# Pairwise distances in a graph layer: from two small matmuls on TensorE to squares on ScalarE and sums on GpSimd, with the messages one graph later

## The chip, the cores and the metric

The kernel runs on one core of one Trainium2 chip. The metric is the device time of one execution in microseconds. Before the change the median of three runs is 2149.64 us (2147.59 to 2150.93).

## The reference

Input x is 64 graphs of 256 nodes with 256 features (fp32), adj is 64 dense 256 x 256 adjacency matrices. Two layers follow each other, each with a residual sum and a layer norm. The first normalizes adj by its row sums and computes (norm_adj + alpha I) x W^T + b. The second, cut to what matters here:

```python
h = relu(bn(conv1d_1tap(x)))                 # 256 -> 256
h = bn(conv1d_17taps(h))                     # along the nodes
x_conv = relu(h + x)
s = x @ w_se.T + b_se                        # three numbers a node
dist = sq[:, :, None] + sq[:, None, :] - 2 * s @ s.T
A = exp(-dist) * adj
msg = relu(x @ w_msg.T + b_msg)
x_nmp = A @ msg
out = GRU(input=[x_conv, x_nmp], state=x)    # w_ih (768 x 512), w_hh (768 x 256)
```

A layer norm of x + out ends it. dist[n, m] is the squared Euclidean distance of two points with three coordinates each.

## The kernel before

**Stages.** The 64 graphs are taken in four quarters of 16. In the setup stage (to about 284 us) the first quarter's graphs pass through both layers up to the GRU's inputs, beside the preparation of the transformed weights of the 17-tap convolution (`weights`). The convolution runs as a real transform of length 48 in tiles of 32 nodes, for a quarter at once: `p_dft` (L480) transforms each graph, `products` multiplies per frequency with u tiles loaded from memory (L539, `load_u` on SyncE), then `real_transform`, `complex_begin` and `complex_end` transform back on VectorE and `output` writes xc_d. Then the GRU (`gates`, `gru`, L832 on) reads three things for each graph from memory: the convolution's result, x1 and xn_d, which holds x1 transposed in its first half and the messages transposed in its second.

While one quarter's products, inverse transform and GRU run, the next quarter's graphs are begun: `open_ahead` holds V2, a buffer for the transforms of the first 12 (later 6) graphs of that quarter, whose own place VM is still in use. They are copied over by `copies` (L1052).

**One graph.** `graphs` (L960) starts the loads of the graph three ahead, and interleaves three generators piece by piece: `layer1` of this graph, `layer0` of the graph two later (adjacency transposes and degrees; p_hT at L399; p_out at L409 with the layer norm) and `others` (weights, or pieces of a GRU). `PLACES` says which of the other two gets a piece after which piece of layer1. The pieces of layer1 are: x1 transposed (L428), `p_conv` with bias and relu into h (L443 to L447; columns 256 to 258 of h are s), `p_msg` (L464), `p_dft` (L480), the rows, the distances with the product, and the messages.

**The distances.** VectorE copies s four times into `scols` (128 columns, of which 3 and a constant one or the halved negative square sum are used), TensorE transposes both chunks (p_rows, L493), ScalarE and VectorE copy 64 rows each out (`dist_l` L495, `dist_r` L497), TensorE multiplies 32 rows of one with 32 of the other (p_dist, L504), and ScalarE takes exp(2 p + bias) with the negative square sum as bias (L505). VectorE multiplies by the adjacency (L506) and TensorE multiplies by msg (p_nmp, L513). ScalarE copies that into the second half of xn, and one transfer of 512 KB writes xn (L518).

**Order.** The framework's scheduler orders each engine's instructions by a model of when their inputs are ready, and by the order in which the program was traced among those that are. The queues are then fixed: each engine takes its instructions in that order and waits where one isn't ready. Buffers are slots of a pool (`bufs=`): a new tile waits until the readers of the slot's last tile are done. `issue_after` forces an order by hand, and `paced` (L942) uses it: after each instruction given to `mark` it queues pieces of the inverse transform at the rates of L1042, so many per mark. In the first quarter `take(begin, 3)` (L1079) advances the next quarter's graphs by three pieces for each of the 12 steps of the products, before `paced` takes the rest.

## Time and profile before

| | before |
|---|---|
| median of three runs | 2149.64 us |
| the profiled execution's span | 2152.3 us |
| TensorE busy (PE) | 2052.7 us, 9693 matmuls |
| VectorE busy (DVE) | 1581.6 us |
| ScalarE busy (ACT) | 841.9 us |
| GpSimd busy (POOL) | 664.8 us |
| DMA | 298.30 MB, mean 139 GB/s |
| mean granted TensorE clock | 0.990 |

The profile is of one execution, whose span is 2.7 us above the median of the timed runs. A line of the groups reads: line of the kernel, engine, operation, written tile <- read tiles, shapes (partitions x elements), count | busy us, mean ns of one | the engine's idle time just before the group and what ended most of it. A span of a matmul holds its tail, which overlaps the next one, so the mean of a single one is longer than the distance from start to start. In a table of stages the columns are the stretch, its length, and for each engine the busy time and the count, then the granted clock, the DMA engines' mean busy share and GB/s. Timelines give start, length, engine, line, operation, tiles, shapes and count.

### The profile page before, as it was taken

How to read it: one execution, taken by the hardware profiler on the slowest of the kernel's cores; microseconds unless marked ns; L12 is line 12 of the kernel's file. 1: busy time of each engine (PE TensorE's matmuls, PEld its weight loads, DVE VectorE, ACT ScalarE, POOL GpSimd, SP SyncE). 2: the span in 40 equal slices, each digit the busy share in tenths (PEclk: the TensorE clock that was granted, in tenths of full speed). 3: DMA queues.
4: the chain of work that ended last, by engine and by line, in shares of the span. 5: the costliest groups of instructions: out<-in, count | busy, mean ns of one | idle time of the engine just before them, and what ended most of it. 6: DMA issues, size and time to landing. Idle time of an engine off the chain costs nothing.

```text
span 2152.3 us, 28977 instructions
## 1 busy us (share of the span) xinstructions
PE 2052.7 (95%) x9693; PEld 1735.8 (81%) x9693; DVE 1581.6 (73%) x3719; ACT 841.9 (39%) x1857; POOL 664.8 (31%) x640
## 2 busy tenths in 40 slices
PE   7999999887999999899999999999999998999997
PEld 5888788776888888788888888777888887788886
DVE  5555578775568788775656988876566889988887
ACT  4665643456431123445552122446553112222222
POOL 2444310121431244213322133323231123444442
PEclk9999999999999999999999999999999999999999
DMA  4766666434346644233326654324324744443331
GB/s 122 235 196 197 198 194 207 142 132 134 96 146 203 203 110 128 93 112 113 113 94 190 205 157 113 118 98 133 102 88 136 243 116 122 119 102 99 94 84 54
DMA packets 295085, 298.30 MB, mean 139 GB/s; under 512 B 76414, under 2 KB 273618, under 8 KB 294938
## 3 DMA queue, kind: packets, MB, share of 16 engines
q1 hardware_dynamic: 235050, 200.46, 30.9%
q10 hardware_dynamic: 44480, 67.39, 8.8%
q0 software_dynamic: 15408, 28.61, 6.1%
q8 instruction: 77, 1.26, 0.2%
q14 instruction: 70, 0.57, 0.1%
HBM read 193.28 MB, written 103.06 MB: 138 GB/s over the span
## 4 chain that ended last, share of the span: by engine, by line
PE 44%; DVE 12%; issue 9%; POOL 6%; ACT 4%; DMA 2%; ACTq 0%; SPq 0%; POOLq 0%; DVEq 0%
PE p_rz L846 14%; PE p_n L883 8%; PE p_k L539 7%; PE p_out L409 2%; PE p_nmp L513 2%; PE p_hT L399 2%; PE p_dft L480 2%; POOL ln_rs L323 2%; PE p_conv L443 1%; PE p_msg L464 1%; PE p_dist L504 1%; POOL sums L826 1%; POOL sums L825 1%; DMA u<-ud 1%; POOL xc_g L796 1%
## 5 line engine op out<-in xcount | busy, mean ns | idle before, releaser
L883 PE MATMUL p_n<-wn,inputs 128*128 128x256 f32 x1536 | 355.1, 385 | 13.4 <-DVE first L859 13.2
L846 PE MATMUL p_rz<-wrz,sums 128*128 128x256 f32 x1536 | 348.6, 380 | 1.3 <-DVE gn L888 0.8
L883 PEld LDWEIGHTS p_n<-wn,inputs 128*128 128x128 f32 x1536 | 288.5, 192 | 64.2 <-DVE first L859 20.9
L846 PEld LDWEIGHTS p_rz<-wrz,sums 128*128 128x128 f32 x1536 | 290.0, 190 | 44.5 <-issue 5.2
L846 PE MATMUL p_rz<-wrz,inputs 128*128 128x256 f32 x1152 | 271.6, 379 | 1.0 <-ACT inputs L808 1.0
L323 POOL TENSOR_TENSOR ln_rs<-ln_rs,neg_half 128x2 f32<-128x2 f32 x129 | 99.1, 768 | 510.9 <-DVE ln_rs L322 464.0
L846 PEld LDWEIGHTS p_rz<-wrz,inputs 128*128 128x128 f32 x1152 | 217.6, 190 | 31.1 <-ACT inputs L808 1.2
L895 ACT ACTIVATE nn<-gn 128x256 f32<-128x256 f32 x128 | 53.3, 417 | 332.1 <-DVE gn L892 331.7
L539 PE MATMUL p_k<-u,VM 128*128 128x256 f32 x736 | 175.2, 380 | 2.7 <-DMA u<-ud 1.9
L369 POOL TENSOR_TENSOR dis<-deg,neg_half 128x2 f32<-128x2 f32 x64 | 46.1, 720 | 423.6 <-DVE deg L367 393.1
L333 ACT ACTIVATE x_g<-x_g,ln_mr,ln_rs 128x256 f32<-128x256 f32 x128 | 70.0, 593 | 241.5 <-DVE ln_mr L331 241.5
L539 PEld LDWEIGHTS p_k<-u,VM 128*128 128x128 f32 x736 | 138.1, 190 | 24.4 <-DMA u<-ud 4.1
L480 PE MATMUL p_dft<-fwd,h 128*128 128x240 f32 x512 | 120.2, 379 | 25.9 <-ACT h L447 24.6
L399 PE MATMUL p_hT<-adjT,x 128*128 128x256 f32 x512 | 129.8, 397 | 14.0 <-DVE adjT L381 7.6
L825 POOL TENSOR_TENSOR sums<-inputs 128x384 f32<-128x384 f32 x64 | 67.1, 1048 | 239.0 <-ACT inputs L816 206.3
L480 PEld LDWEIGHTS p_dft<-fwd,h 128*128 128x128 f32 x512 | 95.2, 192 | 47.6 <-ACT h L447 41.2
L506 DVE TENSOR_TENSOR aT<-aT,adjT 128x512 f32<-128x512 f32 x64 | 44.6, 698 | 118.2 <-ACT aT L505 118.1
L443 PE MATMUL p_conv<-wc,xn 128*128 128x259 f32 x512 | 125.8, 388 | 4.3 <-ACT xn L429 4.3
L392 POOL TENSOR_TENSOR x_t<-x_t,b_t 128x512 f32<-128x512 f32 x64 | 85.4, 1334 | 142.6 <-ACT x L391 97.4
L409 PE MATMUL p_out<-w,hT 128*128 128x256 f32 x512 | 123.1, 383 | 1.4 <-ACT hT L404 0.7
L464 PE MATMUL p_msg<-wmsg,xn 128*128 128x256 f32 x512 | 121.4, 380 | 0.0
L513 PE MATMUL p_nmp<-aT,msg 128*128 128x256 f32 x512 | 121.2, 379 | 0.2 <-DVE aT L506 0.2
(157 smaller groups left out, 3910.2 us busy)
## 6 DMA issues: line engine op xcount, KB each, us to landing
u<-ud SPq DMA_DIRECT2D x284, 256.0 KB
xn_d<-xn ACTq DMA_DIRECT2D x64, 512.0 KB
inputs<-xn_d SPq DMA_DIRECT2D x64, 512.0 KB
ud<-u_set POOLq DMA_DIRECT2D x39, 480.0 KB, 6.1
adj_t<-in_adj_dram SPq DMA_DIRECT2D x64, 256.0 KB
x_t<-in_x_dram SPq DMA_DIRECT2D x64, 256.0 KB
x_d<-x ACTq DMA_DIRECT2D x64, 256.0 KB
xc_d<-VM SPq DMA_DIRECT2D x64, 256.0 KB
```

The costliest lines, as they stand in the source:

```text
L323: nc.gpsimd.tensor_tensor(rs[:, : len(chunks)], rs[:, : len(chunks)], neg_half[:, : len(chunks)], op=ALU.pow)
L392: nc.gpsimd.tensor_tensor(x_t, x_t, b0_t.unsqueeze(1).to_broadcast([P, NCH, D]), op=ALU.add)
L399: nc.tensor.matmul(p[:, k, :], x1[:, mc, k * P : (k + 1) * P], adjT[:, mc, 1 - mc : 3 - mc, :].rearrange("p n q -> p (n q)"), start=mc == ...
L409: nc.tensor.matmul(p[:, c, :], hT[:, k, c * P : (c + 1) * P], w0[:, k, :], start=k == 0, stop=k == DCH - 1)
L443: nc.tensor.matmul(p, x1T[:, k, c * P : (c + 1) * P], wc1[:, k, :], start=k == 0, stop=k == DCH - 1)
L464: nc.tensor.matmul(p[:, c, :], x1T[:, k, c * P : (c + 1) * P], wmsg[:, k, :], start=k == 0, stop=k == DCH - 1)
L480: nc.tensor.matmul(p[:, t0 * FL : t1 * FL], h[:, c, k * P : (k + 1) * P], fwd[:, first : first + t1 - t0, :].rearrange("p t f -> p (t f)") ...
L513: nc.tensor.matmul(p[:, k, :], msg[:, mc, k * P : (k + 1) * P], aT[:, mc].rearrange("p n q -> p (n q)"), start=mc == 0, stop=mc == NCH - 1,)
L539: nc.tensor.matmul(p[:, j * D : (j + 1) * D], v[:, k, :], u[:, k, :], start=k == 0, stop=k == DCH - 1)
L825: nc.gpsimd.tensor_tensor(S[:, 0], A21, A22, op=ALU.add)
L846: nc.tensor.matmul(p[:, j * D : (j + 1) * D], a[:, k], wrz[:, b, k], start=k == 0, stop=k == HALF - 1)
L883: nc.tensor.matmul(p[:, o * D : (o + 1) * D], lhsT, w, start=j == 0, stop=j == len(part) - 1)
```

## The change

The distances are computed directly as a sum of three squares. The three s columns of a graph are copied out of h (`own`), written to memory (s_d, 3 KB) and read back to all 128 partitions as one row of 256 x 3 (`everyone`, 384 KB in all). For each coordinate d and each half of the nodes ScalarE computes (own - everyone)^2 with own as bias and scale -1, six activations of 128 x 256, reading every third element. GpSimd adds the second and the third coordinate to the first. ScalarE takes exp(-aT), VectorE multiplies by the adjacency as before. scols, its transposes, the copies, p_dist and the square sums are gone.

The product with msg runs in the next graph's layer1 (`messages`, after that graph's p_msg), and for the last graph in `graphs`. There x1 of the next graph is transposed too, for every graph (before: only for graphs in ALONE, the others at the beginning of their own layer1). xn is split into x1T and nmp, written by two transfers, both issued by ScalarE's queue.

layer1 has four pieces instead of seven, and PLACES has four entries. Buffers: adjT 4 instead of 3, msg 2 instead of 1, turn 2 instead of 3; V2 of the later quarters holds 5 graphs instead of 6. `everyone`, `aT`, `square` and `nmp` have one buffer each.

```diff
--- before.py
+++ after.py
@@ -140,10 +140,6 @@
     nc.vector.tensor_scalar(alpha_t, alpha_t, MIN_ALPHA, None, op0=ALU.max)
 
 
-    scols = const.tile([P, NCH, P], F32, name="scols")
-    nc.gpsimd.memset(scols, 0.0)
-    for c in (NSE, 32 + NSE):
-        nc.gpsimd.memset(scols[:, :, c : c + 1], 1.0)
 
 
 
@@ -338,8 +334,8 @@
     xc_d = [dram.tile([Q, N, D], F32, name=f"xc_d{q}") for q in range(NQ)]
     x1_d = [dram.tile([Q, N, D], F32, name=f"x1_d{q}") for q in range(NQ)]
     xn_d = [dram.tile([P, 2 * DCH, N], F32, name=f"xn_d{g}") for g in range(B)]
-    XN = {}
-    ALONE = set()
+    s_d = [dram.tile([N, NSE], F32, name=f"s_d{g}") for g in range(B)]
+    X1T, NMP = {}, []
     ADJT, X1, X_SCALED, DIAGONAL = {}, {}, {}, {}
 
 
@@ -347,7 +343,7 @@
 
         a_t, x_t = ain.pop(g), xin.pop(g)
 
-        adjT = work.tile([P, NCH, 3, P], F32, name="adjT", bufs=3)
+        adjT = work.tile([P, NCH, 3, P], F32, name="adjT", bufs=4)
         ADJT[g] = adjT
 
         deg = small.tile([P, NCH], F32, name="deg")
@@ -420,21 +416,58 @@
         yield
 
     def x1_transposed(g):
+        if g >= B:
+            return
         x1 = X1.pop(g)
-        xn = XN[g] = work.tile([P, 2 * DCH, N], F32, name="xn")
+        x1T = X1T[g] = work.tile([P, DCH, N], F32, name="x1T")
         p = bank("p_x1T").rearrange("p (k n) -> p k n", k=DCH)
         for k in range(DCH):
             for c in range(NCH):
                 nc.tensor.transpose(p[:, k, c * P : (c + 1) * P], x1[:, c, k * P : (k + 1) * P], ident)
-        nc.scalar.copy(xn[:, :DCH], p)
+        nc.scalar.copy(x1T, p)
+        nc.scalar.dma_start(xn_d[g][:, :DCH], x1T)
+
+    def adjacency(g, own, adjT, msg):
+
+
+        everyone = work.tile([P, N, NSE], F32, name="s_all", bufs=1)
+        nc.sync.dma_start(s_d[g].rearrange("(c p) s -> p c s", p=P), own)
+        flat = s_d[g].rearrange("n s -> (n s)")
+        nc.sync.dma_start(everyone, bass.AP(tensor=flat.tensor, offset=flat.offset, ap=[[0, P], [NSE, N], [1, NSE]]))
+        yield
+        aT = work.tile([P, NCH, N], F32, name="aT", bufs=1)
+        for d in range(NSE):
+            to = aT if d == 0 else work.tile([P, NCH, N], F32, name="square", bufs=1)
+            for c in range(NCH):
+                nc.scalar.activation(
+                    to[:, c], everyone[:, :, d], AF.Square, bias=own[:, c, d : d + 1], scale=-1.0
+                )
+            if d:
+                nc.gpsimd.tensor_tensor(aT, aT, to, op=ALU.add)
+        nc.scalar.activation(aT, aT, AF.Exp, scale=-1.0)
+        blocks_of = aT.rearrange("p c (n q) -> p c n q", q=P)
+        mark(nc.vector.tensor_mul(blocks_of, blocks_of, adjT[:, :, 0:3:2, :]))
+        NMP.append((g, aT, msg))
+
+    def messages():
+        if not NMP:
+            return
+        g, aT, msg = NMP.pop(0)
+        p = bank("p_nmp").rearrange("p (k n) -> p k n", k=DCH)
+        for k in range(DCH):
+            for mc in range(NCH):
+                nc.tensor.matmul(
+                    p[:, k, :], msg[:, mc, k * P : (k + 1) * P], aT[:, mc], start=mc == 0, stop=mc == NCH - 1,
+                )
+        nmp = work.tile([P, DCH, N], F32, name="nmp", bufs=1)
+        nc.scalar.copy(nmp, p)
+        nc.scalar.dma_start(xn_d[g][:, DCH:], nmp)
 
     def layer1(g, place):
 
-        if g not in XN:
+        if g not in X1T:
             x1_transposed(g)
-        xn, adjT = XN.pop(g), ADJT.pop(g)
-        x1T = xn[:, :DCH]
-        yield
+        x1T, adjT = X1T.pop(g), ADJT.pop(g)
 
         h = work.tile([P, NCH, D + NSE], F32, name="h", bufs=1)
         for c in range(NCH):
@@ -444,20 +477,13 @@
                     p, x1T[:, k, c * P : (c + 1) * P], wc1[:, k, :], start=k == 0, stop=k == DCH - 1
                 )
             mark(nc.vector.tensor_tensor(h[:, c, :], p, bc1, op=ALU.add))
+        own = small.tile([P, NCH, NSE], F32, name="own")
+        nc.vector.tensor_copy(own, h[:, :, D:])
         nc.scalar.activation(h[:, :, :D], h[:, :, :D], AF.Relu)
-
-        s3 = h[:, :, D:]
-        cols = scols.rearrange("p c (q r) -> p c q r", r=32)
-        nc.vector.tensor_copy(cols[:, :, :, :NSE], s3.unsqueeze(2).to_broadcast([P, NCH, 4, NSE]))
-        sq3 = small.tile([P, NCH, NSE], F32, name="sq3")
-        nc.vector.scalar_tensor_tensor(sq3, s3, -1.0, s3, op0=ALU.mult, op1=ALU.mult)
-        nsq = small.tile([P, NCH], F32, name="nsq")
-        nc.vector.tensor_reduce(nsq, sq3, AX.X, ALU.add)
-        nc.vector.tensor_scalar(
-            cols[:, :, 2:4, NSE], nsq.unsqueeze(2).to_broadcast([P, NCH, 2]), 0.5, None, op0=ALU.mult
-        )
-        yield
-        msg = work.tile([P, NCH, D], F32, name="msg", bufs=1)
+        msg = work.tile([P, NCH, D], F32, name="msg")
+        weighing = adjacency(g, own, adjT, msg)
+        next(weighing)
+        yield
         p = bank("p_msg").rearrange("p (c d) -> p c d", c=NCH)
         for c in range(NCH):
             for k in range(DCH):
@@ -466,6 +492,9 @@
                 )
         mark(nc.vector.tensor_tensor(msg, p, bmsg_t.unsqueeze(1).to_broadcast([P, NCH, D]), op=ALU.add))
         nc.scalar.activation(msg, msg, AF.Relu)
+        yield
+        messages()
+        x1_transposed(g + 1)
         yield
 
 
@@ -486,36 +515,7 @@
                 TILES[0][:, :, k, place * GT : (place + 1) * GT],
                 p[:, : GT * FL].rearrange("p (t f) -> p f t", f=FL),
             )
-
-        yield
-        p = bank("p_rows")
-        for c in range(NCH):
-            nc.tensor.transpose(p[:, c * P : (c + 1) * P], scols[:, c, :], ident)
-        dl = work.tile([64, N], F32, name="dist_l", bufs=1)
-        nc.scalar.copy(dl, p[0:64, :N])
-        dr = work.tile([64, N], F32, name="dist_r", bufs=1)
-        nc.vector.tensor_copy(dr, p[64:P, :N])
-        yield
-
-        aT = work.tile([P, NCH, 2, P], F32, name="aT", bufs=1)
-        for c in range(NCH):
-            rows = slice(32 * c, 32 * c + 32)
-            p = bank("p_dist")[:, :N]
-            nc.tensor.matmul(p, dl[rows, c * P : (c + 1) * P], dr[rows, :], start=True, stop=True)
-            nc.scalar.activation(aT[:, c].rearrange("p n q -> p (n q)"), p, AF.Exp, bias=nsq[:, c : c + 1], scale=2.0)
-        mark(nc.vector.tensor_mul(aT, aT, adjT[:, :, 0:3:2, :]))
-        yield
-        if g in ALONE:
-            x1_transposed(g + 1)
-        p = bank("p_nmp").rearrange("p (k n) -> p k n", k=DCH)
-        for k in range(DCH):
-            for mc in range(NCH):
-                nc.tensor.matmul(
-                    p[:, k, :], msg[:, mc, k * P : (k + 1) * P], aT[:, mc].rearrange("p n q -> p (n q)"),
-                    start=mc == 0, stop=mc == NCH - 1,
-                )
-        nc.scalar.copy(xn[:, DCH:], p)
-        nc.scalar.dma_start(xn_d[g], xn)
+        run(weighing)
         yield
 
 
@@ -633,7 +633,7 @@
     def turned(re, im, angle):
 
 
-        t = freq.tile([P, 2, D], F32, name="turn", bufs=3)
+        t = freq.tile([P, 2, D], F32, name="turn", bufs=2)
         x, y = M[:, re, :], M[:, im, :]
         real_part(t[:, int(re > im), :], x, y, angle)
         return imaginary_part(t[:, int(re < im), :], x, y, angle), t
@@ -661,7 +661,7 @@
         nc.vector.tensor_add(M[:, 12, :], M[:, 4, :], M[:, 12, :])
         for i, x, y in ((1, 9, 13), (2, 10, 14), (3, 15, 11)):
             angle = math.pi * ORDER[i] / 8
-            t = freq.tile([P, 2, D], F32, name="turn", bufs=3)
+            t = freq.tile([P, 2, D], F32, name="turn", bufs=2)
             by = real_part(t[:, 0, :], M[:, x, :], M[:, y, :], angle)
             imaginary_part(t[:, 1, :], M[:, x, :], M[:, y, :], angle)
             stt(M[:, 8 + i, :], t[:, 0, :], -by, M[:, i, :], op0=ALU.mult, op1=ALU.add)
@@ -717,7 +717,7 @@
 
         plain = M[:, n // 8 * 8 + ORDER.index(n % 8), :]
         x, y = M[:, re, :], M[:, im, :]
-        t = freq.tile([P, 2, D], F32, name="turn", bufs=3)
+        t = freq.tile([P, 2, D], F32, name="turn", bufs=2)
         by = [real_part(t[:, j, :], x, y, 2 * math.pi * (n + 16 * j) / FL) for j in range(2)]
         yield
         low = min(re, im)
@@ -955,7 +955,7 @@
             yield
 
 
-    PLACES = (("other",), ("layer0",), (), (), ("layer0",), ("other", "layer0"), ())
+    PLACES = (("layer0",), ("other",), ("layer0",), ("other", "layer0"))
 
     def graphs(first, part, others):
 
@@ -969,6 +969,8 @@
                     if next(given[name], "end") != "end":
                         yield
             yield from given["other"]
+            if first + i == B - 1:
+                messages()
 
     with tc.tile_pool(name="setup", bufs=1) as setup:
         load_taps(setup, 0)
@@ -1062,7 +1064,6 @@
                 others = [take(late, 3 if i % 3 == 0 else 2) for i in range(AHEAD)]
             else:
                 others = [nothing() for _ in range(AHEAD)]
-                ALONE.update(range(first, first + AHEAD))
             TILES[0] = V2
             begin = graphs(first, range(AHEAD), others)
         sums(0)
@@ -1096,7 +1097,7 @@
             run(graphs(first, range(AHEAD, Q), others))
             run(early)
             if q == 0:
-                scope, AHEAD, V2 = open_ahead(6)
+                scope, AHEAD, V2 = open_ahead(5)
                 ctx.enter_context(scope)
             late = gates(q, range(EARLY, Q))
         else:
```

## The prediction

> **What bounds the kernel now.** I read the page's busy shares and chain of waits first, then its groups, then the table of stages, last the timelines of single graphs.
>
> ```profile
> PE 2052.7 (95%) x9693; PEld 1735.8 (81%) x9693; DVE 1581.6 (73%) x3719; ACT 841.9 (39%) x1857; POOL 664.8 (31%) x640
> ...
> PE 44%; DVE 12%; issue 9%; POOL 6%; ACT 4%; DMA 2%; ACTq 0%; SPq 0%; POOLq 0%; DVEq 0%
> ```
>
> TensorE is busy for 2052.7 of 2152.3 us, so only 99.6 us of the span are not matmul work. Work taken off TensorE is worth its own time wherever TensorE stays the limit. Four groups of the TensorE list matter:
>
> ```profile
> L504 PE MATMUL p_dist<-dist_r,dist_l 32*128 32x256 f32 x256 | 46.7, 430 | 7.1 <-DVE dist_r L497 6.7
> L493 PE MATMUL p_rows<-ident,scols 128*128 128x128 f32 x128 | 25.2, 279 | 3.8 <-DVE scols L456 3.7
> L480 PE MATMUL p_dft<-fwd,h 128*128 128x240 f32 x512 | 120.2, 379 | 25.9 <-ACT h L447 24.6
> L443 PE MATMUL p_conv<-wc,xn 128*128 128x259 f32 x512 | 125.8, 388 | 4.3 <-ACT xn L429 4.3
> ```
>
> The figure after the second bar is TensorE's idle time just before the group. These four hold 41.1 us of its idle time. The stages differ (columns: PE, PEld, DVE, ACT, POOL busy, clock, DMA share, GB/s):
>
> ```profile
> 30.00:284.00 254.00, 247.59 (x1200) 203.75 (x1200) 140.20 (x372) 152.13 (x356) 104.17 (x99) 0.99 0.61 192
> 390.00:520.00 130.00, 113.68 (x545) 90.31 (x543) 99.66 (x308) 72.57 (x168) 26.60 (x26) 0.99 0.36 120
> 962.00:1150.00 188.00, 185.46 (x904) 155.57 (x904) 113.81 (x305) 99.37 (x231) 61.25 (x62) 1.00 0.36 108
> ```
>
> The first is the setup stage, 16 graphs (15.9 us each, TensorE 97%). The second is nine graphs beside the inverse transform (14.4 us each, TensorE 87%, VectorE 77%): the one stage that TensorE doesn't fill. The third is ten graphs beside four GRU graphs (TensorE 99%). In one graph of it the timeline reads:
>
> ```profile
> 1019.64 1.89 PE L480 MATMUL p_dft<-fwd,h 128*128 128x240 f32 x8
> 1021.37 0.38 PE L493 MATMUL p_rows<-ident,scols 128*128 128x128 f32 x2
> 1021.58 1.89 PE L399 MATMUL p_hT<-adjT,x 128*128 128x256 f32 x8
> 1023.49 0.70 PE L504 MATMUL p_dist<-dist_r,dist_l 32*128 32x256 f32 x4
> 1024.12 2.86 PE L883 MATMUL p_n<-wn,inputs 128*128 128x256 f32 x12
> ```
>
> Ends overlap the next start, so start to start counts: p_rows costs 0.21 us and p_dist 0.63 us.
>
> **What the Trainium skill says.** "TensorEngine Tiling (Array Packing)", section Key Properties: a change of tiling mode drains TensorE. The trace agrees: the eight p_hT matmuls ahead of the 32-row p_dist take 1.91 us start to start, the eight p_out later (1026.81 to 1028.54) 1.73. "ScalarE: Activation LUTs", What ACT_TABLE_LOAD costs: an activation with a per-partition bias takes 280 ns + 0.833 ns an element, 493 ns for 256, and back-to-back ones overlap by 93 ns. The nearest row, L391 with one such operand, has 503 ns mean and 60.4 us for 128, 0.47 each. "SBUF — State Buffer", SBUF: two separate sides: a VectorE instruction with two SBUF inputs and a reading GpSimd instruction lock each other out of a shared port. The trace agrees: the L725 pair at 433.81, beside GpSimd's L392 (433.36, 1.27 us), takes 1.43 us, against 492 ns mean of one.
>
> **The change, part by part.**
>
> 1. TensorE work removed. Start to start 64 x (0.21 + 0.63) = 53.8 us; by busy time 25.2 + 46.7 = 71.9 us, which counts tails and part of the drains. I take the middle, 63 us (0.98 a graph). The messages' eight matmuls stay.
>
> 2. TensorE idle removed. The waits before p_rows and p_dist (3.8 + 7.1) go with their instructions. p_dft waits for the relu of h because only the adjacency transposes and p_msg lie between it and p_conv. Now the previous graph's p_nmp (1.73), the next x1's transposes (0.43) and p_hT (1.73) come between as well, 3.9 us more cover against a typical wait of 24.6/18 = 1.4. And x1T is made most of a graph ahead, which covers the 4.3 us before p_conv. Of the 41.1 us I book 30, since a later ScalarE gives some back.
>
> 3. VectorE. Out: L451, L453, L455, L456, L497 (18.8 + 11.1 + 9.9 + 10.6 + 27.3 = 77.7 us). In: the copy of own, at 0.16 to 0.29 us (L453, L451), 64 times about 14. Net -1.0 us a graph; against that the sums on GpSimd can hold a two-input VectorE instruction for up to their own length. I call VectorE even.
>
> 4. ScalarE. In: six squares at 0.45 (2.7 us) and one 128x512 exp (0.63, as L447). Out: two exps (53.8/64 = 0.84) and the dist_l copy (0.37). Net +2.1 us a graph, 136 us, and one more DMA issue (0.34). The squares read every third float, which no ScalarE row here does: the bounds are 0.40 and, if the stride halves the rate, 0.70 each, so +1.8 to +3.6 us a graph; I take no penalty. ScalarE's share goes from 39% to 46%.
>
> 5. GpSimd. Two 128x512 adds at 1.33 (L392): 2.7 us a graph, 171 us, share 39%. Behind them in its queue stand dis (L369), ln_rs (L323) and the GRU's sums (L825 to L830), each up to 1.33 us later. dis leads to x1 and p_hT, the sums to p_rz: the next TensorE victims.
>
> 6. The DMAs. SyncE gets a write of s (12-byte runs) and, once that has landed, a 384 KB broadcast. The same broadcast exists: bhh (L1009) is issued at 239.47 and its reader L1011 runs at 243.36, so 3.9 us at most. The write appears nowhere; 2.0 (the fixed cost in the skill's "DMA: Bandwidth & Descriptors", Anatomy of one DMA) to 4.4 us (page, xc_g); I take 2.5. So s reaches all partitions 6.4 us after own. SyncE's queue holds load_u, load, load_gate, load_conv and the xc_d writes behind that wait: TensorE waits for u if these slip (now 3.0 us). Outside the transform stages they run well ahead, so I book nothing; uncovered it is 2.5 us a time for the five graphs beside products, 12 us. The bytes are 25 MB on 298.
>
> 7. The chain. Four squares 1.8, add 1.33, two squares 0.9 (they wait for the add, as "square" is one buffer), add 1.33, exp 0.63, product 0.70: 6.7 us, 7.3 with handovers. With the DMAs aT is ready 13.7 us after own. The messages ask for it one graph later, 14.4 us and more, so the latency is hidden, by some 2 us in the second stage and 5 in the third. But ScalarE, if nothing is put between, stands still for 2 x 1.4 = 2.8 us behind the adds.
>
> 8. What that does per stage. Setup: ScalarE 9.5 + 2.1 + 2.8 = 14.4 us a graph against TensorE's 15.5 - 1.0 = 14.5: level, so half of its gain is lost, 16 x 0.5 = 8 us. Second stage: 8.1 + 4.9 = 13.0 against 11.6 for TensorE and 14.4 now: I give back 1.5 us on each of nine, 14 us. The other 39 graphs have room; 0.4 us each for late relus, hT copies and dis, 16 us.
>
> 9. Regrouping. A graph's generator now yields seven times instead of ten, so the 36 steps taken beside the first quarter's products reach 5.1 graphs instead of 3.6; fewer are left to pace the inverse transform (6.9 x 6 marks x 1.2 = 50 of its 70 pieces, before 60). Ten pieces of about 0.7 us come after them: 7 us, once. One graph ahead fewer in later quarters moves a graph from a stage at 94% to one at 99%; nothing. Fewer turn buffers: VectorE alone uses them; nothing. Wider buffers for adjT and msg: the 0.76 us that degrees waits for the product goes, off the path.
>
> Sum: -63 - 30 + 8 + 14 + 16 + 7 = -48. The profiled execution is 2152.3 us, 2.7 above the median, so 2149.6 - 48 = **2102 us**.
>
> **The rivals.**
>
> *ScalarE's queue is blocked (slower).* The squares stand in order ahead of the relu of h, the hT copy and the transform's copies. If the broadcast comes later than the order assumes, all of these wait, then TensorE. For it: VectorE today stands 118 us waiting for aT at L506 (1.85 a graph) in an order that put it too early, and the new chain is three times as long. Against: four PSUM banks let TensorE run about 2 us ahead. The gains are 93 us, 1.45 a graph; from that stall on the change loses. At 2.0 a graph: 2149.6 - 93 + 128 = 2185.
>
> *GpSimd becomes the late one.* Its adds push dis and the sums; every TensorE wait by 0.7 us on 64 graphs and 7 of regrouping leave 2149.6 - 93 + 45 + 38 (steps 8) + 7 = 2147, no measurable change. Against: L323 stands idle before it for 511 us, so its queue has room.
>
> *Everything is hidden.* Only the regrouping is paid and all 41 us of idle go: 2149.6 - 72 - 41 + 7 = 2044; with half of step 8, 2063. For it: TensorE at 99% in the third stage. Against: the second stage.
>
> That the change doesn't do what it says can't be: the instructions are gone. Only their replacement's place in the queues is open.
>
> **From this to the numbers.** Under 0.2% (4 us) this kernel can't be told from no change. The likeliest case, 2075 to 2133, has 0.48; nearly all hidden, below 2075, 0.10; no change 0.07; ScalarE blocked 0.27; slower for a dearer stride, a slower write or the regrouping, 0.08. So faster 0.58, same 0.07, slower 0.35. The range, 2060 to 2190, leaves out the ends of the first and the last cases.
>
> **What would show it.** Right: p_rows and p_dist gone, TensorE busy near 1990 us, its idle before p_dft under 10 us, squares near 0.45 us, ScalarE near 980, GpSimd near 836, a graph of the third stage 1 us shorter. Wrong: ScalarE idle before the squares on the broadcast or on GpSimd for over 2 us a graph, and TensorE idle before p_hT, p_out or p_dft; squares of 0.7 us; VectorE waiting longer than 118 us for the product; u loads late by more than 12 us.

## The result, and the profile after

The changed kernel takes 2394.19 us (median, 2389.11 to 2399.86). The kernel before takes 2148.61 us beside it, so the ratio is 1.1146, with a 95% interval of 1.1119 to 1.1172: 246 us slower. The prediction forecast a gain, to 2102 us with a range up to 2190. The profiled execution of the changed kernel has a span of 2387.3 us. Line numbers in this part are those of the changed kernel.

Busy shares and the chain of waits, from the page of the changed kernel:

```profile
PE 2075.1 (87%) x9309; PEld 1767.1 (74%) x9309; DVE 1519.5 (64%) x3463; ACT 1020.2 (43%) x2113; POOL 831.8 (35%) x765
...
PE 8%; issue 4%; DVE 4%; POOL 3%; ACT 1%; DMA 1%; ACTq 0%; POOLq 0%; SPq 0%; DVEq 0%
```

TensorE has 384 matmuls fewer and is busy longer, 2075.1 us against 2052.7. TensorE and VectorE are less full than before (95% and 73%), ScalarE and GpSimd a little fuller (39% and 31% before), so no engine has become the full one. The chain's shares add up to about 21% of the span, so it is followed only part of the way back and doesn't name the cause here. The waits do. Groups of the changed kernel (after the first bar busy us and mean ns of one, after the second the engine's idle us before the group and what ended it):

```profile
L490 PE MATMUL p_msg<-wmsg,x1T 128*128 128x256 f32 x512 | 150.1, 445 | 89.9 <-DVE x L410 88.9 <-ACT adjT L375 1.1
L459 PE MATMUL p_nmp<-aT,msg 128*128 128x256 f32 x512 | 150.3, 445 | 87.7 <-DVE aT L449 74.6 <-DVE h L479 9.4 <-ACT adjT L375 3.6
L509 PE MATMUL p_dft<-fwd,h 128*128 128x240 f32 x512 | 122.8, 383 | 19.1 <-ACT nmp L463 18.0 <-ACT inputs L816 1.0
L442 ACT ACTIVATE square<-s_all,own 128x256 f32<-128x256 f32 x256 | 151.0, 635 | 109.7 <-DMA s_all<-s_d 57.8 <-POOL aT L446 51.9
L446 POOL TENSOR_TENSOR aT<-aT,square 128x512 f32<-128x512 f32 x128 | 164.1, 1282 | 509.7 <-ACT square L442 405.1 <-ACT aT L442 72.7 <-DMA u<-ud 14.8
L449 DVE TENSOR_TENSOR aT<-aT,adjT 128x512 f32<-128x512 f32 x64 | 49.0, 766 | 164.2 <-ACT aT L447 164.2
```

TensorE's idle time, summed over all its gaps, goes from 88 to 301 us. Of the added 213 us, 178 stand before p_msg and p_nmp. The same two in the kernel before:

```profile
L464 PE MATMUL p_msg<-wmsg,xn 128*128 128x256 f32 x512 | 121.4, 380 | 0.0
L513 PE MATMUL p_nmp<-aT,msg 128*128 128x256 f32 x512 | 121.2, 379 | 0.2 <-DVE aT L506 0.2
```

Both now wait for VectorE. Each wait of over 0.2 us can be followed back along VectorE's queue to the last place where VectorE stood for as long. Of p_msg's 89 us, 60 come from the product that waits for the exp, ahead of L410, and 25 from the sums of u_set that wait for ScalarE's copies. Of p_nmp's 75 us behind the product, 26 come from the product's own wait for the exp. Another 41, in nine waits, come from a layer norm ahead of the product: it waits for ln_rs on GpSimd, and ln_rs stands there behind the adds, which wait for ScalarE's squares. So ScalarE's delays travel on through the queues of VectorE and GpSimd. ScalarE's own waits in the changed kernel (us in total, times, longest):

```profile
ACT aT L447 <- POOL aT L446: 103.9, 63, 3.3
...
ACT aT L442 <- DMA s_all<-s_d: 84.4, 30, 6.5
```

With the two releasers in the group of the squares this is 142 us for the broadcast (84.4 + 57.8) and 156 us for the sums on GpSimd (103.9 + 51.9). The kernel before has neither; its exps wait 10.0 us in all, for p_dist.

SyncE's queue stands as well. It waits for the write to land before it issues the broadcast, with loads behind it:

```profile
SPq L436 <- DMA s_d<-own: 180.4, 63, 4.6
```

TensorE doesn't pay for that: it waits 7.2 us for loads, and 10.0 before the change. VectorE's waits for loads grow from 4 to 65 us; no run prices these alone.

The rest of the loss is matmuls that take longer: without 71.9 us of removed work and with 213 us of new idle time, 235 - 213 + 72 = 94 us of the longer span are busy time. p_msg and p_nmp have a mean of 445 ns instead of 380 and 379, and their busy time grows from 121.4 and 121.2 us to 150.1 and 150.3, 58 us together. The setup stage of the changed kernel (columns as in the table of stages above) shows TensorE at 78% where it was at 97%, with a granted clock of 0.91 instead of 0.99:

```profile
30.00:359.00 329.00, 256.60 (x1102) 207.70 (x1103) 121.87 (x302) 198.60 (x416) 144.90 (x129) 0.91 0.60 169
```

Over the whole span the clock is 0.943 instead of 0.990. The Trainium skill, "TensorE: Matmul & The Clock Gate", section What's actually happening, says that activity releases the throttle. The runs agree in direction: of the versions below, e4, with 82 us of TensorE's idle time, has 0.988, and h2, with 345 us, has 0.930.

One graph of the setup stage shows the order (timeline of the changed kernel: start us, duration us, engine, and in brackets the idle time before):

```profile
203.24 0.19 DVE L481 COPY own<-h 128x6 f32<-128x6 f32 x1
...
203.46 0.38 SPq L434 DMA_DIRECT2D s_d<-own  x1
...
207.75 0.35 SPq L436 DMA_DIRECT2D s_all<-s_d  x1
...
213.09 0.64 ACT L442 ACTIVATE aT<-s_all,own 128x256 f32<-128x256 f32 x1 [1.24 <-DMA s_all<-s_d]
...
215.59 1.05 ACT L301 COPY u_set<-p_u 120x512 f32<-120x512 f32 x2
...
215.78 1.27 POOL L446 TENSOR_TENSOR aT<-aT,square 128x512 f32<-128x512 f32 x1 [5.04 <-ACT square L442]
217.01 3.33 POOL L304 TENSOR_TENSOR u_set<-u_set,u_set 120x1024 f32<-120x1024 f32 x1
220.30 1.26 POOL L446 TENSOR_TENSOR aT<-aT,square 128x512 f32<-128x512 f32 x1
...
216.68 1.45 DVE L303 TENSOR_TENSOR u_set<-u_set,u_set 120x1024 f32<-120x1024 f32 x1 [9.13 <-ACT u_set L301]
218.05 0.86 DVE L410 SCALAR_TENSOR_TENSOR x<-p_out,dis,x_t 128x256 f32<-128x256 f32 x2
...
218.97 1.99 PE L490 MATMUL p_msg<-wmsg,x1T 128*128 128x256 f32 x8 [1.18 <-DVE x L410]
...
221.59 0.63 ACT L447 ACTIVATE aT<-aT 128x512 f32<-128x512 f32 x1 [2.52 <-POOL aT L446]
...
222.26 0.69 DVE L449 TENSOR_TENSOR aT<-aT,adjT 128x512 f32<-128x512 f32 x1 [3.01 <-ACT aT L447]
...
223.09 1.96 PE L459 MATMUL p_nmp<-aT,msg 128*128 128x256 f32 x8 [2.13 <-DVE aT L449]
```

Two chains run through ScalarE's queue. The copies of p_u (L301) stand behind the squares, and so come late. VectorE waits 9.13 us for them, L410 stands behind that on VectorE, and p_msg waits for L410. Further on, the exp waits for the second add. GpSimd put a u_set sum of 3.33 us between the two adds, and product and p_nmp follow only then. From the end of own to the start of the product the median is 18.3 us over the 64 graphs and 19.2 us over the 16 of the setup stage, where a graph takes 21.4 us (15.9 before).

### The profile page after: what moved, and what is told of

Read it like the earlier page. It is cut to its first block, busy times and chain, and to the rows that moved or that the text cites. A ratio compares the mean times of both kernels' runs of the same rounds, so it can differ in the third digit from the quotient of the medians.

```text
span 2387.3 us, 28886 instructions
## 1 busy us (share of the span) xinstructions
PE 2075.1 (87%) x9309; PEld 1767.1 (74%) x9309; DVE 1519.5 (64%) x3463; ACT 1020.2 (43%) x2113; POOL 831.8 (35%) x765
## 5 line engine op out<-in xcount | busy, mean ns | idle before, releaser
L883 PE MATMUL p_n<-wn,inputs 128*128 128x256 f32 x1536 | 357.2, 387 | 18.3 <-DVE first L859 18.3
L883 PEld LDWEIGHTS p_n<-wn,inputs 128*128 128x128 f32 x1536 | 297.1, 195 | 63.1 <-DVE first L859 21.7
L446 POOL TENSOR_TENSOR aT<-aT,square 128x512 f32<-128x512 f32 x128 | 164.1, 1282 | 509.7 <-ACT square L442 405.1
L490 PE MATMUL p_msg<-wmsg,x1T 128*128 128x256 f32 x512 | 150.1, 445 | 89.9 <-DVE x L410 88.9
L459 PE MATMUL p_nmp<-aT,msg 128*128 128x256 f32 x512 | 150.3, 445 | 87.7 <-DVE aT L449 74.6
L442 ACT ACTIVATE square<-s_all,own 128x256 f32<-128x256 f32 x256 | 151.0, 635 | 109.7 <-DMA s_all<-s_d 57.8
L459 PEld LDWEIGHTS p_nmp<-aT,msg 128*128 128x128 f32 x512 | 111.0, 223 | 116.9 <-DVE aT L449 41.9
L490 PEld LDWEIGHTS p_msg<-wmsg,x1T 128*128 128x128 f32 x512 | 108.2, 221 | 115.6 <-DVE x L410 97.3
L395 PE MATMUL p_hT<-adjT,x 128*128 128x256 f32 x512 | 137.0, 411 | 14.4 <-DVE adjT L377 7.6
L888 DVE TENSOR_TENSOR gn<-p_n,bn_t 128x512 f32<-128x512 f32 x128 | 87.3, 682 | 91.5 <-PE p_n L883 91.5
L476 PE MATMUL p_conv<-wc,x1T 128*128 128x259 f32 x512 | 127.4, 391 | 14.7 <-DVE x L410 6.2
```

The source lines that it names most:

```text
L395: nc.tensor.matmul(p[:, k, :], x1[:, mc, k * P : (k + 1) * P], adjT[:, mc, 1 - mc : 3 - mc, :].rearrange("p n q -> p (n q)"), start=mc == ...
L442: nc.scalar.activation(to[:, c], everyone[:, :, d], AF.Square, bias=own[:, c, d : d + 1], scale=-1.0)
L446: nc.gpsimd.tensor_tensor(aT, aT, to, op=ALU.add)
L459: nc.tensor.matmul(p[:, k, :], msg[:, mc, k * P : (k + 1) * P], aT[:, mc], start=mc == 0, stop=mc == NCH - 1,)
L476: nc.tensor.matmul(p, x1T[:, k, c * P : (c + 1) * P], wc1[:, k, :], start=k == 0, stop=k == DCH - 1)
L490: nc.tensor.matmul(p[:, c, :], x1T[:, k, c * P : (c + 1) * P], wmsg[:, k, :], start=k == 0, stop=k == DCH - 1)
```

## The experiments

The medians, with the ratio to the kernel before on the same chip (there its median was 2146.4 to 2148.9 us, so differences between runs of different chips are good to some 2 us). Each is the median of two to five executions, that of e4 of nineteen:

| run | us | ratio, 95% interval |
|---|---|---|
| before | 2148.6 | |
| after | 2394.2 | 1.1146 [1.1119, 1.1172] |
| e1, squares read a resident row, no transfers | 2262.0 | 1.0534 [1.0505, 1.0562] |
| e2, transfers kept, but not waiting for s | 2262.2 | 1.0534 [1.0506, 1.0563] |
| k1, e1 with adds that nobody waits for | 2143.3 | 0.9972 [0.9961, 0.9984] |
| i1, e1 without adds | 2104.7 | 0.9797 [0.9779, 0.9814] |
| f5, e1 with one coordinate | 2089.1 | 0.9729 [0.9696, 0.9762] |
| e4, the new order with the old distances | 2143.3 | 0.9978 [0.9968, 0.9989] |
| e3, after, product on GpSimd | 2407.5 | 1.1211 [1.1177, 1.1246] |
| f1, after, product a graph later | 2367.4 | 1.1025 [1.0971, 1.1078] |
| f4, e1, product a graph later | 2238.0 | 1.0423 [1.0371, 1.0474] |
| w1, after, one more hop through memory | 2402.1 | 1.1193 [1.1161, 1.1225] |
| l1, after, adds on VectorE | 2288.4 | 1.0662 [1.0643, 1.0682] |
| f2, after, squares a graph later | 2170.7 | 1.0109 [1.0074, 1.0144] |
| h1, f2 with coordinates one after the other | 2378.8 | 1.1096 [1.1063, 1.1130] |
| h2, h1, two square buffers, four ahead | 2456.4 | 1.1453 [1.1426, 1.1481] |
| i2, f2, squares and nmp share two buffers | 2213.5 | 1.0307 [1.0290, 1.0324] |
| j2, f2, four graphs ahead | 2191.6 | 1.0207 [1.0191, 1.0222] |
| j1, j2 with two square buffers | 2183.9 | 1.0169 [1.0154, 1.0184] |
| k2, f2 with adds on VectorE | 2130.7 | 0.9910 [0.9893, 0.9926] |

One caution holds for nearly all of these comparisons. The scheduler orders the queues anew for each edit. Of ScalarE's 1984 activations and copies, the longest sequence that a run has in common with the changed kernel is 1742 for e1, 1760 for w1 and 1799 for l1. k1 shares 1674 with e1 and 1926 with i1. So a difference between two runs is that of the edit together with the order that the scheduler made for it. Only h1 has exactly the order of its base (f2), on ScalarE, VectorE and GpSimd.

**The broadcast: e1 and e2.** e1 loads a row once and leaves out both transfers; e2 keeps both, but the read takes its row from x, which is there from the start.

```diff
-        nc.sync.dma_start(s_d[g].rearrange("(c p) s -> p c s", p=P), own)
-        nc.sync.dma_start(everyone, bass.AP(tensor=flat.tensor, ...))
+        everyone = resident        # e1 (e2: transfers kept, read from x)
```

> The kernel after, without the two transfers of the s columns: the squares of every graph read one row of 768 numbers that is loaded once at the start, so the distances are wrong and nothing of the compute instructions is left out. Loop theory: from own to the product a graph takes 18.3 us (median of the trace after), 9.7 of them in the write and the read, and VectorE's queue has the product of a graph ahead of the next graph's sums into h, so that this latency is paid once a graph. Without the transfers own to product is 8 to 9 us, below TensorE's 14.5 us a graph: 2090 to 2200 us, TensorE idle under 140 us. Load theory (squares of 0.64 us on ScalarE and the adds on GpSimd set the pace): above 2340. Regrouping theory (four pieces, messages later, five graphs ahead): above 2300.

> The kernel after, with both transfers, but the 384 KB broadcast reads 768 numbers of the input x in place of s_d, so it waits for the squares of the previous graph and no longer for the write (the distances are wrong; all instructions stay). Loop theory: the write's 4.15 us (median from its issue to the read's issue) and the wait for own leave the loop: 2130 to 2300 us, own to product 4 us or more shorter. If the transfers as traffic are what costs, and not the wait: above 2340.

Both take 2262 us: 132 us less than the changed kernel, and equal. So the traffic of the transfers costs nothing that can be measured, and without the wait for s the time is 132 us lower, against 142 us of ScalarE's wait. The other 114 us of the loss stay, so e1 lies in none of its three ranges. The waits of e1 show ScalarE still behind the adds, 138 us, and TensorE still behind L412, the old L410:

```profile
ACT aT L446 <- POOL aT L445: 81.1, 61, 2.5
...
PE p_msg L489 <- DVE x L412: 69.4, 29, 6.2
...
ACT square L441 <- POOL aT L445: 56.7, 63, 4.9
```

**The order alone: e4.** All of the regrouping, with messages a graph later and five graphs ahead, but scols, p_rows and p_dist as before.

```diff
-        for d in range(NSE): ... squares on ScalarE, adds on GpSimd
+        p_rows, dist_l, dist_r, p_dist, exp     (as in the kernel before)
```

> The kernel after in its new order (messages a graph later, x1 transposed a graph ahead, four pieces, five graphs ahead, the buffers of after), with the distances of the kernel before: row transposes after the messages, distance matmuls after the transform. Loop theory: the order alone costs nothing and covers the waits before the transform (25.9 us in before): 2090 to 2150 us. Regrouping theory: the order is what costs, above 2280.

2143 us, a little below the kernel before. The new order costs nothing, and p_dft's wait falls from 25.9 to 4.4 us (group of e4):

```profile
L521 PE MATMUL p_dft<-fwd,h 128*128 128x240 f32 x512 | 117.7, 374 | 4.4 <-ACT nmp L476 4.4
```

**Load or wait: f5, i1, k1.** All three start from e1. f5 computes one coordinate (two squares, no adds). i1 has six squares and no adds. k1 has the adds too, each of a square buffer to itself, and the exp reads the first coordinate alone.

```diff
-        for d in range(NSE):
+        for d in range(1):                                        # f5
-                nc.gpsimd.tensor_tensor(aT, aT, to, op=ALU.add)   # i1: gone
+                nc.gpsimd.tensor_tensor(to, to, to, op=ALU.add)   # k1, square bufs=2
```

> No transfers (resident row), and only the first of the three coordinates: two squares, no adds on GpSimd, exp and product as in after; the distances are wrong and two thirds of the squares are left out. If the second half of the loss is the chain or the load of squares and adds: 2090 to 2170 us. If it is the regrouping or the product's place in VectorE's queue alone: 2230 to 2270.

> The kernel without the transfers of s (the squares read a row that stays in SBUF, as in the run with the resident row), and without the two adds on GpSimd: all six squares a graph are still made on ScalarE, at the same place in its queue, but the exp reads the first coordinate's squares alone (the distances are not the reference's: one coordinate of three, of a fixed row). Two theories for the 114 us that the resident row left between 2262 and the kernel before. Theory A, ScalarE stands behind GpSimd's adds (156 us of its idle time in the changed kernel, 138 with the resident row): without the adds that wait is gone, ScalarE reaches the next graph's exp, relu and layer-norm in time, and the time is 2090 to 2150 us. Theory B, the load: four more squares of 0.64 us a graph on ScalarE delay what is queued behind them whether it waits or not: 2200 to 2262 us, as with the resident row.

> The kernel without the transfers of s, all six squares on ScalarE and both adds on GpSimd at their place, but nobody waits for the adds: each adds a buffer of squares to itself, the two coordinates have a buffer each, and the exp reads the first coordinate's squares alone (the distances are not the reference's, as without the adds; the squares read a resident row of 64 nodes four times over). With ScalarE standing behind the adds: 2262 us; without the adds: 2105. If the 157 us between them are ScalarE's waits, this run takes 2100 to 2130 us. If they are the load of the adds on GpSimd (dis and ln_rs later in its queue) or on the port that it shares with VectorE, 2200 to 2265.

These settle the second half. From f5 to i1 four squares a graph cost 15.6 us, though they keep ScalarE busy for 136 us more (1005.8 against 869.7). From i1 to k1 the adds as a load on GpSimd cost 38.6 us, with what they do to VectorE (the product there has a mean of 737 ns in i1 and 922 in k1). From k1 to e1, where ScalarE waits for the adds, it is 118.7 us more. In k1 the exp no longer comes late either, nor the product and p_nmp after it (p_nmp's wait is 1.4 us in k1 and 35.3 in e1); the run doesn't separate this from ScalarE's standing. k1's number is outside both ranges that were expected of it: the wait is the larger part, the load a real one. Its adds (group of k1) run at their place, for their length:

```profile
L447 POOL TENSOR_TENSOR square<-square 128x512 f32<-128x512 f32 x128 | 141.1, 1105 | 277.1 <-ACT square L441 275.9
```

k1 also differs from e1 in a second square buffer and in a row of 64 nodes read four times, and its order is nearer to that of i1 than to that of e1, so the split of the 157 us is good to what these do; the squares take 637 ns in k1 and 640 in e1. i1, with all of ScalarE's new load and neither wait, is at 2104.7 us, its page at

```profile
PE 1994.5 (95%) x9309; PEld 1721.7 (82%) x9309; DVE 1516.1 (72%) x3463; ACT 1005.8 (48%) x2113; POOL 676.6 (32%) x637
```

**VectorE's product: e3, f1, f4.** The product stands on VectorE ahead of the next graph's h. e3 moves it to GpSimd; f1 traces it in `messages` instead, behind h; f4 does that in e1.

```diff
-        mark(nc.vector.tensor_mul(blocks_of, blocks_of, adjT[:, :, 0:3:2, :]))
+        nc.gpsimd.tensor_tensor(blocks_of, blocks_of, adjT[:, :, 0:3:2, :], op=ALU.mult)   # e3
+        NMP.append((g, aT, msg, adjT))      # f1, f4: product in messages()
```

> The kernel after, with the product of the exp and the adjacency on GpSimd in place of VectorE. Loop theory, closed by VectorE's queue: nothing of the chain stands in VectorE's queue any more, so the next graph's h no longer waits for it: 2150 to 2300 us, and VectorE's 164 us of waiting for the exp are gone. If ScalarE's queue closes the loop just as well (its squares wait 142 us for the broadcast): above 2330. Load theory (GpSimd gets another 1.3 us a graph): above 2387.

> The kernel after, with only the product of the exp and the adjacency traced later: in messages(), just ahead of p_nmp, so that in VectorE's queue it stands behind the next graph's sums into h. Everything is computed. Theory A (VectorE's queue closes the loop): own to own of a graph falls by several us, 2130 to 2260 us. Theory B (ScalarE's queue closes it: the squares wait there for the broadcast with the next graph's relu and hT copy behind them): the place of the product changes nothing, 2340 to 2400.

> No transfers of the s columns (the squares read one resident row, so the distances are wrong) and the product traced in messages(). What is left is the load of squares and adds and the order of ScalarE's queue. If the second half of the loss (2262 against 2149 us without transfers) is the product in VectorE's queue: 2090 to 2180. If it is the load or ScalarE's and GpSimd's order: 2230 to 2270.

Moving it to GpSimd doesn't help, and putting it later gives 27 us, and 24 in e1. The product's place on VectorE is a small part, and f1 and f4 lie in the ranges given for a cause elsewhere; e3 lies above both of its upper bounds and doesn't tell them apart. In e3 p_nmp waits 99.2 us for the product on GpSimd; in f1 it waits 100 us for VectorE's product. That the product is late wherever it stands fits an exp that is late.

**Latency: w1.** One more transfer of 3 KB between the write and the broadcast.

```diff
+        nc.sync.dma_start(s_e[g], s_d[g])
-        flat = s_d[g].rearrange("n s -> (n s)")
+        flat = s_e[g].rearrange("n s -> (n s)")
```

> The kernel after, with one more transfer of 3 KB in the way of the s columns (memory to memory, then the broadcast); everything is computed. Loop theory: another write with its landing, some 4 us, is paid once a graph in the stages whose pace the loop sets, 64 x 3 to 4: 2560 to 2650 us. If the latency of the transfers is hidden and after is slow for another reason: below 2420.

The time grows by 8 us, where a latency paid once a graph would have cost 64 times the hop. That form of the theory fell. ScalarE's wait for the broadcast is 110 us here, below the 142 of the changed kernel: the order written for w1 has the squares later in ScalarE's queue. The time doesn't fall with this wait, because the delay shows at the end of the chain instead: from own to the product the median in the setup stage is 23.9 us (19.2 in the changed kernel), and p_nmp waits 114.9 us (87.7).

**The adds on VectorE, alone: l1.**

```diff
-                nc.gpsimd.tensor_tensor(aT, aT, to, op=ALU.add)
+                nc.vector.tensor_tensor(aT, aT, to, op=ALU.add)
```

> The changed kernel, full computation, with one edit: the two adds on VectorE instead of GpSimd, everything else in the order of the change. If the two waits in ScalarE's queue add up, the wait for the sums (156 us) shrinks to about a third and the load on GpSimd (39 us) goes, while the wait for the broadcast (142 us) stays: about 2394 - 100 - 39 = 2255 us, 2220 to 2290. If VectorE, itself held up by ScalarE, comes to the adds too late, they wait in turn: 2330 to 2420 us.

2288 us, 106 less, at the upper end of the range. The waits of l1: the broadcast's stay, 145 us, and those for the sums fall from 156 to 67 us (56.3, and 10.8 before the squares). GpSimd's load and those waits go together here.

```profile
ACT aT L442 <- DMA s_all<-s_d: 90.3, 40, 4.9
ACT aT L447 <- DVE aT L446: 56.3, 59, 3.8
ACT square L442 <- DMA s_all<-s_d: 54.2, 13, 7.6
```

**Squares a graph later: f2, and on from it k2.** f2 runs squares, sums, exp and product of a graph in the next graph's layer1, and its messages two graphs later; the last graphs are finished in `graphs`. k2 adds l1's edit to it.

```diff
+        WEIGHING.append(weighing)
+        if len(WEIGHING) > 1:
+            run(WEIGHING.pop(0))      # the graph before
-        run(weighing)
```

> The kernel after, with the squares, sums, exp and product of a graph traced one graph later (after the next graph's p_msg) and its messages two graphs later. Everything is computed. The broadcast is there long before its squares. Theory A and B alike (the transfers' latency in a queue's order): as with the transfers taken away or lower, 2150 to 2265 us; ScalarE's waits for the broadcast below 20 us. If the transfers' latency were still in a loop through the one buffer of the broadcast: above 2330.

> The full computation with squares a graph later and messages two graphs later (2170.7 us), with the two adds on VectorE instead of GpSimd. An add takes about 0.75 us there instead of 1.35, so ScalarE's wait for the sums (127 us there) falls by a third or more if VectorE comes to them in time; VectorE gets 128 instructions, some 95 us more. If the waits of ScalarE are what is left, 2145 to 2165 us; if VectorE's queue is late instead (it is the nearest to full in the second stage), 2175 to 2230 us.

f2 gets back 224 of the 246 us by order alone, with all instructions of the change. It moves both the squares and the messages, and no run separates the two. The waits of f2: the broadcast has mostly landed when the squares come up (30 us are left of 142, where below 20 were expected), and the sums still hold ScalarE for 127 us:

```profile
ACT aT L447 <- POOL aT L446: 71.2, 60, 5.3
ACT square L442 <- POOL aT L446: 55.5, 50, 5.7
ACT square L442 <- DMA s_all<-s_d: 29.0, 19, 3.0
```

ScalarE thus still stands for 157 us in f2. Yet f2 is only 27 us above k1, which has the same squares and adds, no transfers of s and neither wait. TensorE waits 19.9 us before p_msg and 2.6 before p_nmp, where it was 89.9 and 87.7. So a wait in ScalarE's queue has no fixed price: in this order 157 us cost some 27, by this comparison, and in e1's order 138 us cost 118.7.

k2 takes 2130.7 us, 0.9% below the kernel before: 0.991 [0.9893, 0.9926]. An add takes 0.71 us on VectorE instead of 1.35 on GpSimd, and ScalarE's wait for the sums is 57 us. k2 is 40 us below f2, about what the adds cost as a load on GpSimd (38.6 us from i1 to k1), so it doesn't show what the shorter wait is worth. Its waits:

```profile
ACT square L442 <- DMA s_all<-s_d: 43.0, 38, 5.5
ACT aT L447 <- DVE aT L446: 37.3, 52, 6.8
ACT square L442 <- DVE aT L446: 19.8, 31, 2.1
```

**Attempts on f2 that missed: h1, h2, i2, j1, j2.** h1 stores the coordinates one after the other, so that squares read neighbouring floats. h2 adds a second square buffer and opens four graphs ahead. i2 lets `square` and `nmp` share two buffers. j2 opens four ahead, and j1 also has two buffers for the squares.

```diff
-                    to[:, c], everyone[:, :, d], AF.Square, bias=own[:, c, d : d + 1], scale=-1.0
+                    to[:, c], everyone[:, d, :], AF.Square, bias=own[:, d, c : c + 1], scale=-1.0   # h1, h2
+        ... name="square", tag="scratch", bufs=2      # i2, and nmp likewise
+        ... name="square", bufs=2                     # j1, h2
+                scope, AHEAD, V2 = open_ahead(4)      # j1, j2, h2
```

> f2_squares_later with the three coordinates written to memory one after the other (pieces of 4 bytes in the write), so that the squares read consecutive elements; everything is computed. If the step of three elements is what makes a square last 0.63 us: about 0.50 each, ScalarE 0.8 us a graph less, 2130 to 2160 us. If not: squares of 0.63 us again and 2165 to 2180.

> h1_unit_stride with two buffers for the square, so that the third coordinate's squares don't wait for the first add, and for room 4 instead of 5 graphs ahead in later quarters; everything is computed. If ScalarE's standing still behind the add (56 us in f2) costs: 5 to 30 us below h1, 2100 to 2150. If it doesn't: as h1.

> The full computation, as in the run with squares a graph later and messages two graphs later (2170.7 us), but the squares' buffer and the buffer of the VectorE product share one tag of two buffers, so that the third coordinate's squares need not wait until GpSimd's first add has read the buffer. If ScalarE's standing behind the first add is what is left of the loss (127 us of ScalarE's idle time there are ended by GpSimd), about half of that wait goes and the time is 2140 to 2165 us, below or at the kernel before. If it costs nothing there, 2166 to 2175 us. If the shared buffers make the squares wait for VectorE's product instead, 2175 to 2230 us.

> The full computation, squares a graph later and messages two graphs later as in the run of 2170.7 us, with two buffers of their own for the squares, so that the third coordinate's squares wait neither for GpSimd's first add nor for a transfer; the room comes from opening four graphs ahead instead of five. ScalarE's idle time ended by GpSimd should fall from 127 us to about 60. If ScalarE's standing behind the adds is what is left of the loss in that run, 2140 to 2160 us; if it is not on the path there, 2166 to 2180 us. The run with four ahead and one buffer, beside this one, gives the price of the buffer of the opened graph alone.

> As the run of 2170.7 us with squares a graph later, but four graphs opened ahead instead of five and still one buffer for the squares: the control for the two buffers. One graph moves from the stage of the inverse transform to a fuller one; 2166 to 2185 us, and the difference to the run with two buffers is what the second buffer is worth.

h1 does make the squares shorter, 500 ns against 639, but loses 208 us to f2: the write now has pieces of 4 bytes instead of 12, the broadcast is issued 12.8 us after the write in the setup stage (9.3 in f2), and ScalarE stands 292 us for these transfers in all, against 30. As all three queues have f2's order, this is the cleanest price of a wait: 263 us more of it cost 208 us, though ScalarE is busy for 52 us less. TensorE's waits for u, whose loads SyncE issues too, are part of this: 29 us against 5. The largest group of ScalarE's waits in h1:

```profile
L442 ACT ACTIVATE square<-s_all,own 128x256 f32<-128x256 f32 x256 | 119.0, 500 | 330.8 <-DMA s_all<-s_d 263.2 <-POOL aT L446 54.0 <-DMA s_d<-own 10.2
```

h2 inherits this (301 us of the same wait); why it takes another 78 us isn't shown. i2 halves ScalarE's wait for the sums (127 to 63 us) and puts another in its place: a square's buffer comes free only when the transfer of nmp has read it. The wait, from i2:

```profile
ACT square L442 <- DMA xn_d<-nmp: 46.0, 31, 4.3
```

j2 shows that opening four graphs ahead instead of five costs 21 us here. The second buffer is worth 8 us against j2, and not by the mechanism that was expected: ScalarE's wait for the sums stays at 126 us, where 60 were expected. In j1 it is all before the exp (126.1 us). In j2 it is split between the exp (70.3) and the third coordinate's squares (57.2). Both runs lie above their ranges. The second buffer moved the wait to the next instruction that needs the same sum; of these runs only k2, with a shorter sum, made it smaller without putting another in its place.

## Why the prediction was wrong

The ladder from f5 up gives the loss term by term: f5 is 59.5 us below the kernel before; four squares a graph add 15.6, the adds as a load 38.6, the wait for them 118.7, the wait for the broadcast 132.2. That is 305.1 up from f5 and so 245.6 above the kernel before, by construction the whole difference. What it shows is the size of each, in this sequence and with the orders that the scheduler made.

*Step 1 was right, where nothing stands in the way.* TensorE's busy time falls by 70 us in f5 (1982.5) and 58 in i1; 63 was booked.

*Step 2 was right about the place and wrong about the sum.* p_dft's wait fell to 4.4 us in e4 and f5, p_conv's to 0.7. But other waits took their place. TensorE's idle time in all is 82 us in e4, 94 in f5 and 101 in i1, against 88 before, so the 30 us booked were not gained in any run. In the changed kernel p_dft waits 19.1 us, p_conv 14.7 instead of 4.3.

*Step 3 was right in size*: VectorE's busy time fell by 62 us, 1.0 a graph.

*Step 4 mis-sized the squares* (0.635 us, not 0.45, though inside its bounds), so ScalarE is busy for 1020 us, not 980. That term costs little: from f5 to i1 four squares a graph add 15.6 us. i1, with all of ScalarE's load, takes 2104.7 us. That this is near the predicted 2102 is a coincidence: i1 has no adds, no transfers and neither wait, and it lacks step 2's gain.

*Step 5 was right in size*: adds of 1.28 us for 1.33, GpSimd 832 us for 836. What they push on GpSimd costs up to 39 us (k1 against i1), near the 45 of the rival "GpSimd becomes the late one"; the likeliest case booked only a part of its 16 us for late relus, hT copies and dis.

*Step 6 was short*: from own to the first squares 10.0 us in the median over the graphs, not 6.4. The broadcast is issued 4.15 us after the write (2.5 taken, bounds 2.0 to 4.4) and its reader starts 5.9 us after that (3.9 taken, as the most). The lower bound of 2.0 us comes from a section of the skill (Anatomy of one DMA) that describes DMAs issued by GpSimd; this write goes out through SyncE's queue. SyncE's wait was rightly booked at nothing for TensorE: no u load is late.

*Step 7 is the step that failed*, and step 8, which priced it. Step 7 asked when aT is ready for its reader, p_nmp, found it a graph away, and called the latency hidden. Its own sum was short: aT is ready 19.0 us after own in the median, not 13.7, and p_nmp does wait. And the first thing that waits for the broadcast is no reader at the end of the chain: it is ScalarE, which takes its queue in order. A wait in the middle of the chain holds everything behind it, for other graphs too. Step 7 booked nothing for the broadcast and 2.8 us a graph for the adds. ScalarE stands 142/64 = 2.2 us for the first and 156/64 = 2.4 us for the second, so the size of the second was close. Step 8 then took most of it as filled by ScalarE's free time and gave back 8 + 14 + 16 = 38 us. In the order of the change the runs charge 132 + 119 = 251 us for the two waits, nearly their full length (298 us). ScalarE's free share, 57%, didn't absorb them there. In f2's order it stands for 157 us at little cost, so the price lies in what stands behind the wait and how soon that is needed. How much of the 251 us comes through ScalarE's queue alone, and how much through those of VectorE and GpSimd behind it or through the late end of the chain, stays open.

*Step 9* booked 7 us for the regrouping; e4 has all of it and is not slower. Its "nothing" for one graph ahead fewer isn't general: from five to four it was 21 us in f2's order.

*The rivals.* "ScalarE's queue is blocked" named the place, the queue and the point (1.45 us a graph) from which the change loses. It was sized at 2.0 us a graph; with the 4.6 us that the trace shows for the two waits, its own sum gives 2149.6 - 93 + 4.6 x 64 = 2351. The 43 us that are missing are no single term: the gain was 59.5 us in f5 and not 93, the loads of squares and adds cost 54 more, and the waits cost 251 and not 294. "Everything is hidden", 2044 to 2063, was reached by no run; f5, with two thirds of the squares left out, takes 2089. Of the signs of being wrong that the prediction named, ScalarE's idle time before the squares (3.0 us a graph) and VectorE's wait for the product (164 us) came true. TensorE's waits fell on p_msg and p_nmp, which were not among them.

Left open: how much of the 94 us of longer matmuls is the lower clock and how much is how the profile models their ends.

## What to carry to other kernels

When work moves onto an engine that runs its queue in order, ask at each instruction of the chain what it will wait for when its turn comes, what stands behind it, and how soon that is needed; that the end of the chain has time says nothing about its middle. The busy share doesn't answer it: here 136 us of squares cost 16 us, and 298 us of waiting cost 251. Nor does the length of the wait alone: in f2's order 157 us cost some 27. What helped was the place (f2: the squares a graph later, when their input has mostly landed, and the messages two graphs later) and the sum on a faster engine (k2, l1), rather than one more buffer.

## What the runs showed of the hardware

- An activation of 128 x 256 that reads every third float takes 635 to 647 ns, one that reads neighbours 500 (h1): 0.14 us each. The Trainium skill, "SBUF — State Buffer", section Door 1: The DMA port swizzle, says that accesses need two hits in a line of 16 bytes for full bandwidth, and concludes that one can stride for free as far as four fp32. At a step of three fp32, 12 bytes, ScalarE was slower, so the conclusion doesn't hold for this case.
- A write of 3 KB in pieces of 12 bytes lets the dependent read be issued only 4.15 us later in the median, though its last packet has landed 1.7 us after the issue (1.1 to 4.2). The skill's "DMA: Bandwidth & Descriptors", section Anatomy of one DMA, gives about 2.0 us as the fixed cost of a DMA that GpSimd issues; this one, issued by SyncE, took longer. In f2 it was 9.3 us in the setup stage: other issues stand between, and the one buffer of the broadcast comes free late (SyncE waits 104 us for the squares that read it). With pieces of 4 bytes (h1, in the same order) it was 12.8 us, and SyncE waited 338 us for the write, against 84 in f2.
- The product on VectorE has a mean of 690 to 693 ns where no GpSimd instruction of over 0.9 us ran beside it (before, after, e1, i1, k1 and k2). Beside one the mean is longer: 1354 ns for 22 of the 64 in e1, of which one took 2.82 us beside a GpSimd sum of 3.32 us.
